# A graph layer on one core: longer lead-in, sets of three groups of two-part rows

## The chip, the cores and the metric

The kernel runs on one core of a Trainium2 chip. A core has TensorE (PE, matrix products; its weight loads are shown apart as PEld), VectorE (DVE), ScalarE (ACT), GpSimd (POOL), SyncE (SP, which here only issues transfers) and 16 DMA engines that move data between the chip's memory and the core's SBUF. Each engine has one queue of instructions and works through it in order; engines wait for one another by semaphores. Sums of matrix products land in PSUM.

The metric is the device time of one execution, in microseconds, as the median of several runs. Before the change it is 2603.83 us (three runs: 2600.77, 2603.83 and 2609.32).

## The reference

One layer of a graph network: 12500 nodes with 256 features, 200000 edges sorted by their target `dst`. All data is float32.

```python
h = relu(layernorm(x))                          # 12500 x 256, over the features
agg = segment_sum(h[src], dst, num_segments=N)  # one sum for each node
z = (1.0 + eps_gin) * h + agg
t = z @ W1 + b1                                 # 256 -> 512
t = relu(batchnorm(t, g1, bt1))                 # over all nodes
y = t @ W2 + b2                                 # 512 -> 256
out = x + relu(batchnorm(y + h, g2, bt2))       # over all nodes
```

The sources `src` are random, so `h[src]` is a gather of 200000 rows of 1 KB. The batch norms need statistics over all nodes, so all of `t` has to be there before the second layer starts.

## The kernel before

**Sizes.** 128 edges make a tile (1563 tiles, the last of 64 edges), 12 tiles (`GT`, L18) make a group (131 groups). Nodes come in 25 chunks of 512. Since `dst` is sorted and the edges are many, the 1536 edges of a group point at some 96 neighbouring nodes (`STEP`, L71), nearly at a place that can be told in advance; `MARGIN` (L19) is the leeway.

**Index part (L134 to L221).** `dst` and `src` are loaded as blocks of 128 x 128 edges, 13 blocks beside each other (L144, L152), all on SP's queue, and cast by DVE (L161). TensorE transposes them (L166) and DVE copies them out (L168), so that each tile's edges lie down a column of `dstT` and `srcT`. L176 to L185 work out, for each group, its first node and each edge's distance to it. Then the kernel checks that all distances are from 0 to 127 and all leeways fit: three passes of DVE per item (L194 clips, L197 compares, L200 counts). The count becomes a flag that is read into a register; 0 leads into `fast()`, 1 into `general()`, which does not run with these inputs.

**Gather and sum (in `fast()`).** `gather(i)` (L378) issues 12 indirect DMAs on POOL's queue (L383), each fetching 128 rows by 128 indices into a buffer `gt`; there are `AHEAD` + 1 = 5 such buffers (L301). `sums(i)` (L404) builds on DVE twelve 128 x 128 matrices `oh`, with a one where an edge points at a node (L408), and TensorE adds up the rows with them: 12 products 128 x 128 by 128 x 256 into one PSUM tile `ps` (L418). That is the sum for 128 neighbouring nodes, which start at the group's first node. `join(i)` (L423) has ACT copy it to SBUF (`zs`, L425) and DVE build a placing matrix `at` (L427); `put(i)` (L432) has TensorE transpose and shift the sum to its place with two products (L437); `add(i)` (L442) has DVE add that to the columns of `z` (L450). A chunk of `z` begins as the columns of `h`, loaded from `h_cols` (SP, L396) and scaled by 1 + eps on ACT (L397). When a chunk is complete, `first_layer(c)` (L453) multiplies it by W1 in four slices of 512 nodes (L459), takes batch statistics on DVE (L463), copies on ACT (L464) and stores the chunk of `t` by one DMA on ACT's queue (L465).

**Lead-in.** The table of normalized rows, `h_tab`, isn't there at the start. The first `LEAD` = 24 groups therefore gather from `x` itself and are normalized in their buffer after the gather: `settle` (L324) takes the statistics of two tiles at a time on DVE (`bn_stats`, L329), the square root on ACT, and normalizes on ACT tile by tile (L340). Beside this, `h_chunk` (L355) normalizes the rows of a chunk in the same manner, stores them to `h_tab` (ACT's queue), transposes them on TensorE (L366) and stores the columns to `h_cols` (SP). From group 24 on, `gather` reads `h_tab`, whose writes must all have landed.

**Order.** A single loop (L472 to L494) goes over the groups: up to two chunks of `h` as they come due, the gather of group i + 4, copy and placing of group i - 1, sums of group i, addition of group i - 1, first layers that are due. The tile scheduler may reorder within what data and buffers allow; each engine then has a fixed queue.

**Second phase (L513 to L558).** Batch norm of `t`, the second layer (L527) from `t_tab`, its statistics, batch norm and output. It starts when the last group is done.

Of the kernel before, what the change touches and what calls it, by code (L numbers as in the profile page):

```python
# [7 lines left out]
F32 = mybir.dt.float32  # L8
I32 = mybir.dt.int32
AF = mybir.ActivationFunctionType  # L10
OP = mybir.AluOpType
# [7 lines left out]
MARGIN = 76  # L19
AHEAD = 4  # L20
LEAD = 24
# [9 lines left out]
def kernel(  # L31
# [41 lines left out]
    NBLK = -(-max(NTILE, NG * GT) // P)  # L73

# [59 lines left out]
    whole_blocks = full_tiles // P  # L134
    rest = NTILE - whole_blocks * P
    with ExitStack() as es:
        raw = es.enter_context(tc.tile_pool(name="raw", bufs=1))
        ps_t = es.enter_context(tc.tile_pool(name="ps_t", bufs=2, space=PSUM))
        ps_v = es.enter_context(tc.tile_pool(name="ps_v", bufs=2, space=PSUM))
        for name, arr in (("d", dst), ("s", src)):  # L140
            ti = raw.tile([P, NBLK, P], I32, name="rawi_" + name)
            tf = raw.tile([P, NBLK, P], F32, name="rawf_" + name)
            if whole_blocks:
                nc.sync.dma_start(  # L144
                    ti[:, :whole_blocks, :],
                    arr[: whole_blocks * P * P].rearrange("(b p e) -> p b e", p=P, e=P),
                )
            if rest:
                nc.gpsimd.memset(ti[:, whole_blocks, :], 0)
                whole = full_tiles - whole_blocks * P  # L150
                if whole:
                    nc.sync.dma_start(  # L152
                        ti[:whole, whole_blocks, :],
                        arr[whole_blocks * P * P : full_tiles * P].rearrange("(p e) -> p e", e=P),
                    )
                if left:
                    nc.sync.dma_start(
                        ti[whole : whole + 1, whole_blocks, :left],
                        arr[full_tiles * P :].rearrange("(o e) -> o e", o=1),
                    )  # L160
            nc.vector.tensor_copy(tf, ti)  # L161
            for b0 in range(0, NBLK, 4):
                m = min(4, NBLK - b0)
                pt = ps_t.tile([P, 4, P], F32, name="pt")
                for b in range(m):
                    nc.tensor.transpose(pt[:, b, :], tf[:, b0 + b, :], ident)  # L166
                to = dstT if name == "d" else srcT
                nc.vector.tensor_copy(  # L168
                    to[:, b0 * P : (b0 + m) * P], pt[:, :m, :].rearrange("p b e -> p (b e)")
                )  # L170
# [15 lines left out]
        held = raw.tile([P, NG * GT], F32, name="held")  # L186
        odd = raw.tile([P, NG * GT], F32, name="odd")
        cnt = raw.tile([P, 3], F32, name="cnt")
        nc.vector.memset(cnt, 0.0)
        parts = [(rel, 0, P, full_tiles, P), (shift, 0, P, NG, 2 * MARGIN + 1)]  # L190
        if left:
            parts.append((rel, full_tiles, left, 1, P))
        for k, (v, t0, rows, n, end) in enumerate(parts):
            nc.vector.tensor_scalar(  # L194
                held[:rows, :n], v[:rows, t0 : t0 + n], 0.0, float(end - 1), op0=OP.max, op1=OP.min
            )
            nc.vector.tensor_tensor(  # L197
                odd[:rows, :n], held[:rows, :n], v[:rows, t0 : t0 + n], op=OP.not_equal
            )
            nc.vector.reduce_sum(cnt[:rows, k : k + 1], odd[:rows, :n], axis=mybir.AxisListType.X)  # L200
        pc = ps_v.tile([P, 3], F32, name="pc")
        nc.tensor.matmul(pc[:1, :], lhsT=ones, rhs=cnt, start=True, stop=True)
        both = raw.tile([1, 3], F32, name="both")
# [61 lines left out]
    def fast():  # L265
# [24 lines left out]
        with ExitStack() as fs:  # L290
# [7 lines left out]

            with ExitStack() as es:
# [46 lines left out]
                def x_chunk(g):  # L346
# [4 lines left out]
                    if n < CH:  # L351
                        nc.vector.memset(xts[g], 0.0)
# [458 lines left out]
```

## Time and profile before

| | |
|---|---|
| median of three runs | 2603.83 us |
| profiled execution, its own time | 2627.44 us |
| its span | 2625.6 us |
| first gather (of `x`) starts | 32.4 us |
| first gather of `h_tab` starts | 504.8 us |
| last gather ends | 2327.6 us |
| busy: PE / PEld / DVE / ACT / POOL | 1404.3 / 1001.2 / 716.2 / 460.3 / 1484.3 us |
| gathers of `x`: 288 | 273.8 us busy, mean 951 ns |
| gathers of `h_tab`: 1275 | 1208.9 us busy, mean 948 ns |

The profile is of one execution. Its own time, 2627.44 us, is longer than the median of the runs, so a sum of its rows is to be set against 2627, not against 2604. Busy time counts an engine's work without its waits. A gather that POOL issues counts only for the time that POOL prepares it; the transfer runs on the DMA engines. Lines are given as L383 and so on; a releaser is what ended the idle time before an instruction, and "remote" there means that the profile found nobody that did.

A view that cuts the 2625.6 us into 40 slices shows how the work is spread: the lead-in is the first seven to eight slices, then POOL is evenly busy to slice 35, and the second phase takes the rest.

```profile
POOL 4654656666666666666666666566666666630000
...
DMA  5444665433333333333333333333333333328728
```

### The profile page before, as it was taken

Reading aid. Unit: us, or ns where it says so; the run is one execution under the profiler, and the core shown is the slowest. Engines: PE = TensorE matmul, PEld = TensorE weight load, DVE = VectorE, ACT = ScalarE, POOL = GpSimd, SP = SyncE. Lnnn points to the kernel's source line nnn. Section 1 sums busy time; section 2 is a strip of 40 time slices with the busy share of each in tenths; the row PEclk is TensorE's granted clock in tenths of the full one; section 3 lists DMA queues with packets and bytes.
Section 4 is the critical chain, followed back from the end, with each engine's and each line's share of the span. In section 5 each row is a group of like instructions: output and inputs, shape, how many; then the busy total and the mean of one; then the engine's idle time right before and its main releaser. Section 6 shows DMA issues by size and latency. Waiting matters only on the chain.

```text
span 2625.6 us, 14777 instructions
## 1 busy us (share of the span) xinstructions
PE 1404.3 (53%) x4873; PEld 1001.2 (38%) x4873; DVE 716.2 (27%) x1060; ACT 460.3 (18%) x871; POOL 1484.3 (57%) x1575
## 2 busy tenths in 40 slices
PE   1234566645455455445545545544555553578995
PEld 1223344434434334343333424433334442453444
DVE  5234555412212112122111212211121211133444
ACT  1335465510000000000000000000000000013434
POOL 4654656666666666666666666566666666630000
PEclk6666777777777777677777767777777776788996
DMA  5444665433333333333333333333333333328728
GB/s 163 158 152 136 206 199 185 139 114 92 116 119 108 100 120 112 92 116 119 113 92 116 112 94 118 105 120 92 119 110 96 116 114 90 108 77 328 273 82 301
DMA packets 150067, 349.41 MB, mean 133 GB/s; under 512 B 28920, under 2 KB 84366, under 8 KB 143838
## 3 DMA queue, kind: packets, MB, share of 16 engines
q0 software_dynamic: 75008, 204.90, 26.9%
q1 hardware_dynamic: 44182, 91.21, 10.0%
q10 hardware_dynamic: 30792, 52.26, 5.3%
q8 instruction: 41, 0.67, 0.1%
q14 instruction: 44, 0.36, 0.0%
HBM read 284.26 MB, written 64.00 MB: 133 GB/s over the span
## 4 chain that ended last, share of the span: by engine, by line
another core or an unknown queue 50%; PE 25%; issue 10%; ACT 6%; DVE 5%; DMA 3%; POOL 1%; ACTq 0%; SPq 0%; DVEq 0%; POOLq 0%
PE ps L418 9%; PE py L527 6%; PE pz L437 4%; PE ph L459 4%; ACT gt L340 3%; DVE st L463 1%; DMA out_dram<-ot 1%; ACT zs L425 1%; POOL gt L383 1%; ACT ht L340 1%; DVE oh L408 1%; PE po L551 1%; ACT zc L397 1%; DMA zc<-h_cols 1%
## 5 line engine op out<-in xcount | busy, mean ns | idle before, releaser
L383 POOL DMA_INDIRECT gt<-h_tab,srcT x1275 | 1208.9, 948 | 616.4 <-issue 373.8
L418 PE MATMUL ps<-gt,oh 128*128 128x256 f32 x3126 | 767.2, 406 | 88.8 <-ACT gt L340 70.8
L418 PEld LDWEIGHTS ps<-gt,oh 128*128 128x128 f32 x3126 | 648.3, 208 | 206.9 <-ACT gt L340 74.3
L437 PE MATMUL pz<-at,zs 128*128 128x280 f32 x524 | 210.8, 538 | 789.1 <-ACT zs L425 672.0
L408 DVE TENSOR_TENSOR oh<-col,dstT 128x1536 f32<-128x1536 f32 x131 | 229.1, 1749 | 1192.6 <-remote 942.9
L437 PEld LDWEIGHTS pz<-at,zs 128*128 128x128 f32 x524 | 121.6, 248 | 850.2 <-ACT zs L425 693.3
L383 POOL DMA_INDIRECT gt<-in_x_dram,srcT x288 | 273.8, 951 | 196.5 <-ACT zs L425 109.3
L425 ACT COPY zs<-ps 128x256 f32<-128x256 f32 x131 | 48.8, 372 | 1614.0 <-remote 1261.3
L459 PE MATMUL ph<-zc,w1s 128*128 128x512 f32 (+1 forms) x400 | 210.3, 677 | 206.2 <-ACT ts L464 138.2
L459 PEld LDWEIGHTS ph<-zc,w1s 128*128 128x128 f32 x400 | 84.9, 220 | 311.6 <-issue 154.9
L450 DVE TENSOR_TENSOR zc<-pz,zc 128x560 f32<-128x560 f32 (+9 forms) x203 | 100.9, 527 | 315.8 <-remote 189.8
L527 PE MATMUL py<-tT,w2s 128*128 128x512 f32 (+1 forms) x400 | 170.9, 591 | 11.7 <-ACT tT L520 11.7
L340 ACT ACTIVATE gt<-gt,nbg,rsg 128x256 f32<-128x256 f32 x288 | 149.5, 590 | 4.2 <-DVE nbg L338 1.9
L527 PEld LDWEIGHTS py<-tT,w2s 128*128 128x128 f32 x400 | 76.9, 193 | 105.7 <-issue 87.2
L463 DVE BATCH_NORM_STATS2 st<-ph 128x6 f32<-128x512 f32 (+1 forms) x100 | 67.1, 681 | 153.5 <-PE ph L459 60.1
L329 DVE BATCH_NORM_STATS2 stg<-gt 128x6 f32<-128x512 f32 x144 | 91.5, 689 | 34.7 <-DMA gt<-in_x_dram,srcT 22.6
L464 ACT COPY ts<-ph 128x512 f32<-128x512 f32 (+1 forms) x100 | 57.4, 575 | 194.9 <-DVE st L463 150.6
L520 ACT ACTIVATE tT<-ti,of,sc 128x512 f32<-128x512 f32 (+1 forms) x100 | 72.1, 791 | 100.8 <-issue 86.7
L366 PE MATMUL pc<-ident,ht 128*128 128x128 f32 x196 | 38.2, 327 | 66.1 <-issue 27.9
L427 DVE TENSOR_SCALAR at<-col,shift 128x280 f32<-128x280 f32 x131 | 65.5, 500 | 0.3 <-PE pz L437 0.3
L531 DVE TENSOR_TENSOR yT<-py,yT 128x512 f32<-128x512 f32 (+1 forms) x50 | 33.9, 678 | 110.2 <-PE py L527 110.2
L366 PEld LDWEIGHTS pc<-ident,ht 128*128 128x128 f32 x196 | 27.7, 168 | 84.9 <-issue 33.8
(74 smaller groups left out, 393.8 us busy)
## 6 DMA issues: line engine op xcount, KB each, us to landing
t_tab<-ts ACTq DMA_DIRECT2D x24, 1024.0 KB
ti<-t_tab SPq DMA_DIRECT2D x24, 1024.0 KB
gt<-h_tab,srcT POOLq DMA_INDIRECT x1275
xt<-in_x_dram SPq DMA_DIRECT2D x24, 512.0 KB
h_tab<-ht ACTq DMA_DIRECT2D x24, 512.0 KB
h_cols<-hc SPq DMA_DIRECT2D x24, 512.0 KB
zc<-h_cols SPq DMA_DIRECT2D x24, 512.0 KB
yT<-h_cols SPq DMA_DIRECT2D x24, 512.0 KB
```

Source lines behind the costliest of these rows:

```text
L329: nc.vector.bn_stats(st[:, c : c + 2, :].rearrange("p c s -> p (c s)"), v[:, c : c + 2, :].rearrange("p c d -> p d c"),)
L340: nc.scalar.activation(to[:, c, :], v[:, c, :], AF.Relu, bias=nb[:, c : c + 1], scale=rs[:, c : c + 1])
L383: nc.gpsimd.indirect_dma_start(out=ga[:rows, t - t0, :], out_offset=None, in_=x if i < LEAD else h_tab, in_offset=bass.IndirectOffsetOnAxi ...
L408: nc.vector.tensor_tensor(oh[:, :n, :], col[:, :P].unsqueeze(1).to_broadcast([P, n, P]), dstT[:, t0 : t0 + n].unsqueeze(2).to_broadcast([P ...
L418: nc.tensor.matmul(ps, lhsT=oh[:rows, j, :], rhs=ga[:rows, j, :], start=(j == 0), stop=(j == n - 1))
L425: nc.scalar.copy(zs, summed.pop(i))
L437: nc.tensor.matmul(pz[:, d, :WIDE], lhsT=zs[:, d * P : (d + 1) * P], rhs=at, start=True, stop=True)
L450: nc.vector.tensor_add(side, pz[:, :, a - lo : b - lo], side)
L459: nc.tensor.matmul(ph[:, :n], lhsT=w1s[:, d, f * P : (f + 1) * P], rhs=zc[c][:, d, :n], start=(d == 0), stop=(d == DC - 1),)
L463: nc.vector.bn_stats(st1[:, f, c, :], ph[:, :n])
L520: nc.scalar.activation(tT[:, f, :n], ti[:, f, :n], AF.Relu, bias=of1[:, f : f + 1], scale=sc1[:, f : f + 1],)
L527: nc.tensor.matmul(py[:, :n], lhsT=w2s[:, f, d * P : (d + 1) * P], rhs=tT[:, f, :n], start=(f == 0), stop=(f == HC - 1),)
```

## The change

1. **Index part.** A partition now holds 13 x 128 = 1664 edges in a row (`PART`) instead of 13 pieces of 128. `dst` is loaded on SP's queue and cast and copied by DVE; `src` is loaded on ACT's queue and cast and copied by ACT. The check takes, in place of three DVE passes, one ACT pass that sums what lies below zero and one DVE maximum.
2. **Two-part rows.** A new table `h_two` (12500 x 512) takes the place of `h_tab` in `fast()`. Each normalized row is stored as `hi`, its value rounded to float32r, and `lo`, the rest (`ht` - `hi`, also float32r). Main groups gather 2 KB rows of it. Their sums run in float32r over 512 columns, one half for `hi` and one for `lo`; `hold` then adds the two (ACT copies `lo`, DVE adds `hi`). The lead-in's groups sum in float32 over 256 columns as before.
3. **Lead-in of 29 groups** (`LEAD`), in an order written out by hand: per group i, the gather of group i + 4, the addition of group i - 4, copy of the sum of i - 2, the one-hots of i + 1, one chunk of `h`, normalizing of gathered group i + 1, sums of i, transposes of chunk i - 1, placing of i - 2, and one slice of the first layer. The first two main groups are gathered in iterations 26 and 27; the lead-in's buffers then give way to those of the main part.
4. **Sets of three** (`SET`) in the main part, also in a fixed order (`manual_schedule`). A set's three sums lie in three parts of one PSUM tile (`pss`), its one-hots in three parts of `ohs`. Per set: for each of the three groups before, copy and add of the halves; then placing and addition one after the other, with the new set's one-hots and up to three slices of the first layer among them; then the three placing matrices; then the three sums, each followed by the gather five groups ahead (`LOTS` = 5 buffers).
5. **Smaller parts.** `MARGIN` 64 instead of 76 (placing matrices of 256 columns instead of 280); two PSUM tiles for placing instead of one; the first layer's slices are copied into three small tiles and stored one by one (100 DMAs instead of 25); loads of `z`'s columns and their scaling are placed by hand.

The diff, cut to its core:

```diff
-MARGIN = 76
+MARGIN = 64
 AHEAD = 4
-LEAD = 24
+SET = 3
+LEAD = 29
...
+        PART = NBLK * P
+        for name, arr, eng in (("d", dst, nc.sync), ("s", src, nc.scalar)):
...
+                eng.dma_start(ti[:safe, :], arr[: safe * PART].rearrange("(p e) -> p e", e=PART))
...
+                if name == "d":
+                    nc.vector.tensor_copy(columns[:, b0 : b0 + m, :], pt[:, :m, :PU])
+                else:
+                    nc.scalar.copy(columns[:, b0 : b0 + m, :], pt[:, :m, :PU])
...
+            nc.scalar.activation(
+                below[:rows, :n], v[:rows, t0 : t0 + n], AF.Relu, bias=zero[:rows], scale=-1.0,
+                accum_out=cnt[:rows, 2 * k : 2 * k + 1],
+            )
+            nc.vector.reduce_max(top[:rows, k : k + 1], v[:rows, t0 : t0 + n], axis=mybir.AxisListType.X)
...
-                held[:rows, :n], v[:rows, t0 : t0 + n], 0.0, float(end - 1), op0=OP.max, op1=OP.min
...
-                odd[:rows, :n], held[:rows, :n], v[:rows, t0 : t0 + n], op=OP.not_equal
...
-            nc.vector.reduce_sum(cnt[:rows, k : k + 1], odd[:rows, :n], axis=mybir.AxisListType.X)
...
+            h_two = dram.tile([N, 2 * D], F32, name="h_two")
...
-                gat = es.enter_context(tc.tile_pool(name="gat", bufs=AHEAD + 1))
...
+                es.enter_context(tc.manual_schedule())
+                LOTS = 5
...
+                ohs = own.tile([P, SET, GT, P], F32R, name="ohs")
+                pss = psp.tile([P, SET, 2 * D], F32, name="pss")
...
+                    hl = lnp.tile([P, R, 2, D], F32R, name="hl")
+                    hi, lo = hl[:, :n, 0, :], hl[:, :n, 1, :]
+                    nc.scalar.copy(hi, ht[:, :n, :])
+                    nc.vector.tensor_tensor(lo, ht[:, :n, :], hi.bitcast(F32), op=OP.subtract)
+                    carry(
+                        nc.scalar, hl.rearrange("p c s d -> p c (s d)").bitcast(F32), h_two, g, store=True,
+                    )
...
-                            out=ga[:rows, t - t0, :], out_offset=None, in_=x if i < LEAD else h_tab,
+                            out=ga[:rows, t - t0, :], out_offset=None, in_=x if i < LEAD else h_two,
...
+                def bank(i):
+                    return pss[:, i % SET, :D] if i < LEAD else pss[:, i % SET, :]
...
+                def hold(i):
+                    zss[i] = sel.tile([P, D], F32, name="zs", bufs=SET)
+                    if i < LEAD:
+                        nc.scalar.copy(zss[i], bank(i))
+                    else:
+                        nc.scalar.copy(zss[i], bank(i)[:, D:])
+                        nc.vector.tensor_add(zss[i], bank(i)[:, :D], zss[i])
...
+                for i0 in range(LEAD, NG + SET, SET):
+                    here = list(range(i0, min(i0 + SET, NG)))
+                    ripe()
+                    some = pick(SET if here else len(done["slices"]))
+                    for i in before:
+                        hold(i)
+                    scale()
+                    ahead = here[i0 == LEAD :]
+                    for k, i in enumerate(before):
+                        put(i)
+                        add(i)
...
+                        if k:
+                            for j in ahead[:1]:
+                                edges(j)
+                            ahead = ahead[1:]
+                            for c, f in some[:1]:
+                                slice_of(c, f)
+                                take(c, f)
+                            some = some[1:]
...
+                    for i in here:
+                        spots(i)
+                    for i in here:
+                        sums(i)
+                        gather(i + LOTS)
+                    if here:
+                        ready(here[-1])
+                    before = here
```

## The prediction

> **What bounds the kernel now.** I read first the page's chain that ended last and its costliest groups, then the span cut into stretches, then the waits inside the long middle stretch, then its timeline.
>
> ```profile
> another core or an unknown queue 50%; PE 25%; issue 10%; ACT 6%; DVE 5%; DMA 3%; POOL 1%; ACTq 0%; SPq 0%; DVEq 0%; POOLq 0%
> ...
> L383 POOL DMA_INDIRECT gt<-h_tab,srcT x1275 | 1208.9, 948 | 616.4 <-issue 373.8
> L418 PE MATMUL ps<-gt,oh 128*128 128x256 f32 x3126 | 767.2, 406 | 88.8 <-ACT gt L340 70.8
> ```
>
> Half of the chain has no named releaser: this kernel is bound by hand-ons that the profile can't place, not by an engine that is full. The stretches:
>
> ```profile
> 32.00:505.00 473.00, 226.22 (x803) 164.32 (x804) 210.53 (x392) 218.53 (x463) 273.97 (x289) 0.69 0.55 176
> 505.00:2328.00 1823.00, 922.82 (x3298) 690.51 (x3298) 372.33 (x473) 125.46 (x242) 1208.69 (x1275) 0.74 0.36 108
> 2328.00:2625.00 297.00, 248.04 (x743) 140.53 (x742) 117.51 (x166) 114.00 (x165) 0.00 (x0) 0.90 0.62 222
> ```
>
> Columns: stretch, length, busy PE, PEld, DVE, ACT, POOL, granted TensorE clock, DMA share, GB/s. Lead-in 473 us (24 groups), middle 1823 us (107 groups, 17.0 us each), second layer and output 297 us. Which engine sets the 17.0 us? The waits from 700 to 2200 us (engine and line, releaser, total, times, longest):
>
> ```profile
> ACT zs L425 <- remote: 981.2, 51, 30.6
> ...
> POOL gt L383 <- issue: 305.5, 1001, 0.6
> POOL gt L383 <- remote: 181.4, 43, 6.4
> ```
>
> Behind each gather POOL spends 0.30 us more (305.5/1001), so a gather takes 0.949 + 0.305 = 1.254 us and a group of 12 takes **15.04 us**. The other 2 us are stalls of 4.2 us (181.4/43), one for each pair of groups: POOL waits for a buffer. The timeline shows why:
>
> ```profile
> 1246.54 7.08 PEld L418 LDWEIGHTS ps<-gt,oh 128*128 128x128 f32 x24
> 1247.00 7.02 PE L418 MATMUL ps<-gt,oh 128*128 128x256 f32 x24
> ...
> 1264.89 0.81 DVE L450 TENSOR_TENSOR zc<-pz,zc 128x344 f32<-128x344 f32 x2 [18.58 <-remote]
> ...
> 1273.40 1.76 DVE L408 TENSOR_TENSOR oh<-col,dstT 128x1536 f32<-128x1536 f32 x1 [7.29 <-remote]
> 1273.45 0.37 ACT L425 COPY zs<-ps 128x256 f32<-128x256 f32 x1 [28.53 <-remote]
> 1273.63 0.95 POOL L383 DMA_INDIRECT gt<-h_tab,srcT  x1 [6.28 <-remote]
> ```
>
> TensorE's 24 records (a group's last 20, the next one's first 4) end at 1254.0. The copy of that sum, the next one-hots and the gather that reuses the buffer need only these matmuls, and all three start at 1273.4, 19 us later. So while gathers run, what TensorE has done is often seen up to some 20 us late; the trace doesn't say by what. Behind the last gather (2327.6) it stops: sums are copied at 2332.2, 2338.3, 2344.5 and 2350.6, 6.1 us a group. The middle is thus POOL's 15.04 us plus the stalls that late hand-ons make. POOL's floor for all 1563 gathers is 1960 us; first to last they take 2295 us, so 335 us are stalls: 112 in the lead-in (473 - 24 x 15.04), 223 in the middle.
>
> **The change part by part**
>
> *Index part.* L194, L197 and L200 (0.97 + 1.79 + 1.78 us) become one ACT pass beside one DVE reduction of 1.8 us, and src's DMAs leave SP's queue for ACT's. The first gather stands at 32.4 us; I put it at 27, which saves 5 (ends 2 and 10).
>
> *Lead-in, 29 groups instead of 24.* A group now takes 472.4/24 = 19.7 us. Added per chunk: the ACT copy that makes hi (1.15 us, as L397 for 1024 elements) and the DVE subtraction that makes lo (1.2 us, as L557), with the stores twice as wide. Both lie on the round trip between DVE statistics and ACT normalizing, so up to +2.4 us a group. Taken away: copy and placing of a sum come two groups later in the engines' queues, and addition four, so POOL's 99.3 us of waits for the copy at L425 (150 to 500 us) can shrink. The slices of the first layer go one to a group, inside the same idle time. I set loss against gain: 19.7 us (ends 15.04, POOL's floor, and 22.1). The 30th group's gathers stand in iteration 26, behind all row stores, and the pools that give way must be done. They start at 27 + 25 (first group gathered and normalized) + 26 x 19.7 = **564 us**. Now they start near 590, so little is won here.
>
> *Gathers of 102 groups from two-part rows.* There are as many gathers, each of 128 rows, with 2 KB a row instead of 1. The trace has no such gather. The nearest row is the last tile: 64 rows, half the bytes, 0.901 us.
>
> ```profile
> L383 POOL DMA_INDIRECT gt<-h_tab,srcT x1275: 901/949/963, 504.8 to 2326.6; - x183
> ```
>
> Halving rows and bytes saves 0.048 us; if bytes alone carry it, doubling them costs 0.096 us, x 1215 = 117 us. The other end is nothing: as many rows are looked up, and more bytes give no gain. I take a quarter, **30 us**[...].
> Will the DMA engines keep up? 262 KB in 1.254 us are 209 GB/s, beside some 16 of other traffic; slices of this profile reach 328. Here a rule of the Trainium skill speaks against the change: DMA: Bandwidth & Descriptors, Anatomy of one DMA, gives a POOL-issued DMA about 2.0 us plus bytes/436 GB/s, so 2.6 us for 262 KB. Paid one after the other this makes 1215 x 2.6 = 3160 us, 1636 over what I sum. But the same rule gives today's gather 2.3 us, and the trace issues one every 1.254 us a thousand times: the fixed part overlaps, only the 0.6 us of bytes counts. I follow the row.
>
> *Sums in float32r.* A float32 matmul is two records (1563 make 3126). Twelve single ones over 512 columns take 12 x 0.216 to 0.427 = 2.6 to 5.1 us a group, if one goes at the pace of today's records (7.02 us for 24: 0.427 at half clock, 0.216 at full). If float32r runs as float32 does, it is 24 records of 512 columns, 10.4 to 20.5 us. I take the first; POOL's 45.1 us for a set hides it. A second rule speaks against it: TensorE: Matmul & The Clock Gate, HAM oscillation, says that idle stretches over some 3.4 us put TensorE back to half clock, and the change leaves it idle longer. The granted clock is 0.74 in the middle already. Wholly at half clock a set costs 15.4 (sums) + 5.1 (placing) + 10.2 (slices) = 31 us, at full 15.5; both lie under 45.1, so neither alters the sum.
>
> *Sets of three, in a fixed order.* Now each group's placing stands in TensorE's queue inside the next group's sums, so every late hand-on holds back a buffer. Afterwards three sums run, then three placings. A set's ring has two hand-ons in series: sums to copy, and first placing to addition, which frees the buffer for the third placing and lets the one-hots follow; work beside them is some 14 us. Five buffers leave POOL 60 us before it needs the first back. At today's mean lateness (981.2 us over 88 groups: 11 us) the ring takes 2 x 11 + 14 = 36 us, under 45.1; at the worst, 2 x 20.2 + 14 = 54. I allow **30 us** of stalls in all (ends 0 and, one stall of 4.3 in each of 34 sets, 146). The margin of 64, the added DVE addition (102 x 0.4 us) and 75 more stores on ACT's queue (0.33 us each) lie on engines busy 20% and 7% of the middle: nothing. Were this cover gone, the ring would lengthen by 1 to 3 us a set, still under 45.1.
>
> *Tail.* From the last gather's end to the end of the span 298 us; kept.
>
> **Sum:** 564 + 1215 x 1.254 (1523) + 30 + 30 + 298 = 2445 us of span, 2447 with the 1.8 us around it, against the profiled execution's 2627.4: **-180 us**. The median of the runs is 2603.8; 180 off it gives 2424.
>
> **Rivals**
> 1. *Main case:* POOL bounds the middle, with few stalls. 2424 us, own range 2330 to 2500. Chance 0.68.
> 2. *Late hand-ons hold the sets (other side).* Place: from a set's last sum to the next set's one-hots. Price: two hand-ons of 20.2 us make 54.4 us a set, 34 x 9.3 = 316 instead of 30 us, 2710. It decides from 5.3 us more a set (180/34). For it: 20 us waits recur. Against it: POOL's stalls end them, and five buffers reach over them. One 4.3 us stall a set gives 2540 (0.07); the full price, or enough of it, 0.08.
> 3. *The wide gather is dearer.* By the linear end 2511 (0.08). Above 0.17 us each (210 us, with the 30 already in) it is slower; the 64-row gather speaks against that (0.05).
> 4. *float32r at float32's pace.* TensorE then needs 31 + 15 = 46 us a set at full clock, and with the ring's waits some 52: 2424 + 34 x 6 = 2630 (0.04).
>
> Within 0.3% is about what a measurement of this kernel can't tell from no change. Faster 0.80, same 0.03, slower 0.17. Range 2330 to 2600: it leaves out half of the lead-in's gain below, and rivals 2 to 4 at full price above.
>
> **What would show it.** Right: gathers of h_two at 0.95 to 1.0 us, POOL stalls in the middle under 100 us, the 30th group starting at 540 to 590, the middle near 15.3 us a group. Wrong: gathers over 1.1 us, POOL waiting some 4 us in every set or more, sums over 6 us a group, or a lead-in beyond 620 us.

## The result, and the profile after

The changed kernel takes 2639.53 us in the median of four runs (2628.70 to 2660.69), the kernel before 2606.57 us (2600.77 to 2618.10). The ratio is **1.0141**, with a 95% interval of 1.0091 to 1.0191: slower by 1.4%, a small loss, where 180 us less were forecast.

The profiled execution of the changed kernel took 2628.70 us, with a span of 2626.8 us. Its stretches, cut at the first main gather and at the end of the last one (columns as in the prediction: stretch, length, busy PE, PEld, DVE, ACT, POOL, granted TensorE clock, DMA share, GB/s):

```profile
26.00:570.00 544.00, 270.83 (x962) 204.42 (x963) 272.33 (x465) 284.68 (x566) 340.03 (x348) 0.76 0.59 189
570.00:2338.00 1768.00, 641.28 (x1976) 431.24 (x1975) 377.77 (x545) 116.43 (x227) 1148.42 (x1215) 0.67 0.66 197
2338.00:2626.00 288.00, 241.52 (x692) 131.64 (x690) 121.81 (x173) 115.54 (x167) 0.06 (x1) 0.90 0.65 233
```

Set beside the sum that was forecast:

| term | forecast, us | measured, us |
|---|---|---|
| start of the first main gather | 564 | 570.1 |
| 1215 main gathers at POOL's own pace | 1523 | 1519 (0.945 + 0.305 us each) |
| wide rows | +30 | 0 |
| stalls in the middle | +30 | **249** (1768 - 1519) |
| behind the last gather | 298 | 289 |
| span | 2445 | 2627 |

The miss is 182 us, and one row, the stalls, is 219 us over its forecast. The costliest groups of the page show that the gathers themselves became no dearer (a mean of 945 ns, against 948 before) and that the sums became cheap:

```profile
L430 POOL DMA_INDIRECT gt<-h_two,srcT x1215 | 1148.5, 945 | 655.5 <-issue 369.0
...
L475 PE MATMUL pss<-gt,ohs 128*128 128x512 f32 x1215 | 348.2, 445 | 136.9 <-issue 98.7
```

What POOL waited for in the middle (POOL's waits from 570 to 2338 us; releaser, total, times, longest) is again its buffers, which the sums set free. The first line is mainly the 0.305 us behind each gather:

```profile
POOL gt L430 <- issue: 369.0, 1147, 18.7
POOL gt L430 <- remote: 131.8, 25, 7.4
POOL gt L430 <- PE pss L475: 110.1, 14, 18.5
```

And the timeline shows that the hand-on from TensorE comes later than it ever did before:

```profile
1216.90 4.25 PE L475 MATMUL pss<-gt,ohs 128*128 128x512 f32 x12 [1.85 <-issue]
...
1261.66 0.94 POOL L430 DMA_INDIRECT gt<-h_two,srcT  x1 [4.33 <-remote]
1281.77 0.37 ACT L484 COPY zs<-pss 128x256 f32<-128x256 f32 x1 [71.67 <-remote]
1282.01 0.94 POOL L430 DMA_INDIRECT gt<-h_two,srcT  x1 [5.65 <-remote]
```

The set's third sum ends at 1221.15. The copy that needs nothing else starts at 1281.77, 60.6 us later. Two stalls of POOL, of 4.33 and 5.65 us, end together with hand-ons: the first lets POOL's own buffer through, the second the copy. Over the 34 sets, the first copy starts up to 62 us after the last sum; before the change the longest lateness in the middle was 22.8 us. That was no fixed bound: stalls of POOL came more often then (54 over 1 us in the middle, 39 after), and hand-ons come through with a stall.

Side by side, the two profiles have the same span for opposite reasons: the first main gather stands 65 us later (570.1 against 504.8, with five groups more in the lead-in), the middle is 55 us shorter (1768 against 1823, with 60 gathers less), and the tail 9 us. Per main gather the middle takes 1823/1275 = 1.430 us before and 1768/1215 = 1.455 us after. The profile of before is of an execution 21 us above its median, that after of one 11 us below, so the 33 us between the medians can't be divided among the stretches.

### The profile page after: what moved, and what is told of

The parts are those of the page before. It is cut to its first block, busy times and chain, and to the rows that moved or that the text cites. A ratio compares the mean times of both kernels' runs of the same rounds, so it can differ in the third digit from the quotient of the medians.

```text
span 2626.8 us, 12696 instructions
## 1 busy us (share of the span) xinstructions
PE 1160.7 (44%) x3658; PEld 773.1 (29%) x3658; DVE 783.2 (30%) x1210; ACT 525.2 (20%) x975; POOL 1491.6 (57%) x1576
## 4 chain that ended last, share of the span: by engine, by line
another core or an unknown queue 32%; issue 22%; PE 20%; DVE 9%; ACT 6%; POOL 6%; DMA 4%; ACTq 0%; DVEq 0%; POOLq 0%
PE py L693 6%; PE pss L475 6%; POOL gt L430 4%; PE ph L514 4%; ACT gx L369 3%; DVE stg L358 3%; PE pz L496 3%; POOL gx L430 2%; DVE ohs L457 2%; DMA gx<-in_x_dram,srcT 2%; DMA out_dram<-ot 1%; DVE zc L507 1%; ACT ht L369 1%; DVE st L525 1%
## 5 line engine op out<-in xcount | busy, mean ns | idle before, releaser
L430 POOL DMA_INDIRECT gt<-h_two,srcT x1215 | 1148.5, 945 | 655.5 <-issue 369.0
L496 PE MATMUL pz<-at,zs 128*128 128x256 f32 x524 | 171.6, 473 | 863.6 <-DVE zs L485 490.2
L430 POOL DMA_INDIRECT gx<-in_x_dram,srcT x348 | 340.0, 977 | 168.2 <-issue 114.8
L475 PE MATMUL pss<-gt,ohs 128*128 128x512 f32 x1215 | 348.2, 445 | 136.9 <-issue 98.7
L475 PE MATMUL pss<-gx,ohs 128*128 128x256 f32 x696 | 216.9, 485 | 282.1 <-ACT zs L482 164.7
L475 PEld LDWEIGHTS pss<-gt,ohs 128*128 128x128 f32 x1215 | 255.3, 213 | 225.2 <-issue 151.0
L475 PEld LDWEIGHTS pss<-gx,ohs 128*128 128x128 f32 x696 | 172.0, 252 | 336.7 <-ACT zs L482 180.9
L457 DVE TENSOR_TENSOR ohs<-col,dstT 128x1536 fp32r<-128x1536 f32 x131 | 226.5, 1736 | 0.0
L369 ACT ACTIVATE gx<-gx,nbg,rsg 128x256 f32<-128x256 f32 x348 | 174.1, 587 | 14.5 <-DVE nbg L367 9.5
L358 DVE BATCH_NORM_STATS2 stg<-gx 128x6 f32<-128x512 f32 x174 | 107.7, 685 | 11.3 <-DMA gx<-in_x_dram,srcT 11.3
```

Of the source, the lines that this page charges most:

```text
L358: nc.vector.bn_stats(st[:, c : c + 2, :].rearrange("p c s -> p (c s)"), v[:, c : c + 2, :].rearrange("p c d -> p d c"),)
L369: nc.scalar.activation(to[:, c, :], v[:, c, :], AF.Relu, bias=nb[:, c : c + 1], scale=rs[:, c : c + 1])
L430: nc.gpsimd.indirect_dma_start(out=ga[:rows, t - t0, :], out_offset=None, in_=x if i < LEAD else h_two, in_offset=bass.IndirectOffsetOnAxi ...
L457: nc.vector.tensor_tensor(ohs[:, i % SET, :n, :], col[:, :P].unsqueeze(1).to_broadcast([P, n, P]), dstT[:, t0 : t0 + n].unsqueeze(2).to_br ...
L475: nc.tensor.matmul(bank(i), lhsT=oh[:rows, j, :], rhs=ga[:rows, j, :], start=(j == 0), stop=(j == n - 1))
L496: nc.tensor.matmul(pz[:, d, :], lhsT=zs[:, d * P : (d + 1) * P], rhs=at, start=True, stop=True)
```

## The experiments

All of them were held against these theories:

- **A**: while POOL gathers, each hand-on from TensorE is late by itself; a pause of POOL lets it through.
- **B**: the 2 KB rows load the DMA engines and hold things up.
- **C**: TensorE's last update stays behind until TensorE goes on with other work.
- **D**: five buffers are too few, whatever the hand-ons do.
- **E**: the number of hand-ons counts, at a fixed rate.
- **F**: what gathers lead to is worked off at a rate of its own, one in some 1.42 us; POOL issues one in 1.25 us, and TensorE is held up by the surplus. **G**: the same, by the number of gathers and not by their rows.
- **H**: the stalls come from TensorE's own amount of work.

Each experiment is one execution with a profile. Four executions of the changed kernel differ by up to 1.2%, so smaller differences in time say little; the middles of its two profiles agree within 3 us. "Middle" is from the start of the first main gather to the end of the last, and "stalls" is what it takes above POOL's own pace. The kernel before, run beside them on the same chip, took 2594.8 us (first four runs), 2602.8 (next four), 2613.6 (next three), 2266.5 (next four) and 2592.6 us (last three).

### Width of the rows, a pause, no gathers, a busy TensorE

**half_rows.** Main gathers of 1 KB: the low parts of the rows are left out.

```diff
-            h_two = dram.tile([N, 2 * D], F32, name="h_two")
+            h_two = dram.tile([N, D], F32, name="h_two")
...
-                    carry(
-                        nc.scalar, hl.rearrange("p c s d -> p c (s d)").bitcast(F32), h_two, g, store=True,
-                    )
+                    carry(nc.scalar, hl[:, :, 0, :].bitcast(F32), h_two, g, store=True)
...
-                        gathered[i] = pools[k >= 2].tile([P, GT, 2 * D], F32R, name=f"gt{k >= 2:d}")
+                        gathered[i] = pools[k >= 2].tile([P, GT, D], F32R, name=f"gt{k >= 2:d}")
...
-                        nc.scalar.copy(zss[i], bank(i)[:, D:])
-                        nc.vector.tensor_add(zss[i], bank(i)[:, :D], zss[i])
+                    nc.scalar.copy(zss[i], bank(i))
```

> Main groups gather only the hi half: 1 KB rows, sums over 256 columns, one ACT copy; lo is left out of the sums. Theory A (what TensorE finishes is seen late as long as POOL issues gathers back to back, whatever their width; only a stall of POOL lets it through): POOL's stalls in the middle stay near the 248 us of the changed kernel, 2600 to 2640 us, and copies of sums still come tens of us after the last sum. Theory B (the 2 KB rows load the DMA engines and hold things up): stalls fall under 80 us, 2400 to 2460 us.

Measured: 2603.2 us. The middle takes 1765 us, 243 of them above POOL's own pace, and copies still come up to 63 us after the last sum. That is theory A's number; theory B falls. The width may cost something elsewhere: the first main gather stands at 548.9 us, some 20 us earlier than with the wide stores (570.1, and 574.1 in after_again). But the bfloat16 kernels below, whose rows are as narrow, start it at 555 to 587 us, so this isn't shown.

**pool_pause.** POOL does something else for a while behind each set's gathers.

```diff
                     for i in here:
                         sums(i)
                         gather(i + LOTS)
+                    if here:
+                        for _ in range(12):
+                            nc.gpsimd.memset(pad, 0.0)
```

> POOL fills a scratch tile 12 times (about 6 us) behind the gathers of each set of three, 34 sets, 204 us of added POOL work. Theory A, if only gathers do harm: what TensorE did comes through during each pause, POOL's waits for buffers in the middle fall from 248 to under 60 us, 2560 to 2620 us. Theory A, if any work of POOL does it: waits stay, 2780 to 2830 us. Theory B (width of the rows) says nothing of the pause: waits shrink only by what overlaps, 2700 to 2830 us.

Measured: 2629.1 us, neither of the two times for theory A. The pauses of 7.1 us take the place of the waits one for one: POOL's waits for buffers fall to one of 8.5 us, besides one of 18.8 us at the start, and the middle still takes 1764 us. The work that POOL does in a pause counts as rest from gathering. The time, however, is as if the sum of pauses were fixed.

**sp_loads.** The same bytes by SP's queue.

```diff
+                        if i >= LEAD:
+                            r0 = t * 61 % (N - P)
+                            nc.sync.dma_start(ga[:rows, t - t0, :], h_two[r0 : r0 + rows, :])
+                            continue
                         nc.gpsimd.indirect_dma_start(
```

> The main groups are loaded as 128 consecutive rows of the two-part table by SP's queue, one DMA a tile of the same 262 KB, in place of POOL's gathers; which rows are summed is thus not the reference's. Theory A: without POOL's gathers the copy of a set's sums follows its last sum within 3 us throughout, however full the DMA engines are. Theory B: with the same bytes in flight, copies still come more than 10 us after the last sum.

Measured: 2004.4 us. In the waits from 700 to 1700 us the copy of the sums (L488 there) has a named releaser, the sums, and no "remote" at all:

```profile
ACT zs L488 <- PE pss L479: 192.9, 28, 9.2
```

Every copy starts as the set's last product ends. The DMA engines moved 260 GB/s in the mean here, against 198 with gathers. So it isn't full DMA engines that hold TensorE up. The loads differ from the gathers in two things, though, the queue and the rows, which are consecutive and not scattered; the run doesn't tell which of the two counts.

**busy_pe.** TensorE goes on behind the third sum.

```diff
+                        for _ in range(24):
+                            nc.tensor.matmul(
+                                idle, lhsT=w1s[:, 0, :P], rhs=w1s[:, 0, :D], start=True, stop=True
+                            )
                         ready(here[-1])
```

> Behind a set's third sum TensorE makes 24 more products into an unused part of PSUM (48 records of 256 columns, 10 to 20 us), so that it doesn't fall idle with the last sum. Theory C (TensorE's last update stays behind until TensorE goes on): the copy of the sums starts while these products run, within 5 us of the last sum, and POOL's stalls in the middle fall under 100 us, 2440 to 2530 us. Theory A: copies still wait for a stall of POOL, tens of us after the last sum, stalls 220 to 350 us, 2600 to 2730 us.

Measured: 2906.1 us, slower than any theory had it. The copies come at once now, in all sets but one near the start; POOL stalls some 15 us in every set, as the ring has become longer. But the next hand-on is late: the first placing ends at 1229.6 us, TensorE works on until 1234.3, and the addition starts at 1263.9, behind a stall of POOL. So theory C falls.

### Order, buffers, spacing, depth

**early_onehots.** The one-hots ahead of the additions in DVE's queue.

```diff
-                    ahead = here[i0 == LEAD :]
+                    for j in here[i0 == LEAD :]:
+                        edges(j)
...
-                            for j in ahead[:1]:
-                                edges(j)
-                            ahead = ahead[1:]
```

> In the changed kernel, DVE builds the next set's one-hots right behind the copies of the sums, ahead of the additions, which wait for TensorE's placing. Theory A (late hand-ons from TensorE while POOL gathers): the next sums no longer queue behind a second late hand-on on DVE's queue, stalls of POOL in the middle fall from 260 to 120 to 200 us, 2500 to 2570 us. Theory D (five buffers are too few whatever the hand-ons do): 2620 to 2650 us.

Measured: 2627.2 us; 231 us of stalls are left. That misses A's number and meets D's, which the next run tests.

**before_8_buffers.** The kernel before with eight buffers, and main gathers seven groups ahead.

```diff
+MAINAHEAD = 7
...
-                gat = es.enter_context(tc.tile_pool(name="gat", bufs=AHEAD + 1))
+                gat = es.enter_context(tc.tile_pool(name="gat", bufs=2 * AHEAD))
```

> The kernel before, with eight gather buffers in place of five and main gathers seven groups ahead. Theory A: a late hand-on lasts until POOL stalls, so more buffers only put the same stalls off; 2570 to 2610 us, stalls of POOL in the middle still 180 to 240 us. Theory D: POOL runs through the late hand-ons, stalls under 80 us, 2430 to 2480 us.

Measured: 2660.5 us, middle 1815 us, 221 of stalls. Theory D falls for the kernel before. (The 58 us above the kernel before are not in the middle, which took 1823 us in the profile of before.)

**spaced_gathers.** A small fill behind each main gather.

```diff
+                        if i >= LEAD:
+                            nc.gpsimd.memset(pad[:, :P], 0.0)
```

> Changed kernel with a small fill by POOL (128 elements, some 0.2 us) behind each of the 1215 main gathers; POOL's floor grows by 240 to 600 us. If it is the rate of gathers that holds TensorE's hand-ons back: copies follow the last sum within 3 us, no stall over 1 us is left but for a few, total 2627 - 250 + the added fill. If only a pause of several us frees them: late copies of tens of us and stalls stay, total 2627 + most of the fill.

Measured: **2570.2 us**, less than any run of either kernel where TensorE is held up: POOL was given 1215 instructions more and the end came sooner. A gather and its fill take 1.34 us in the median, so POOL's own pace is 105 us slower, and the stalls over 1 us fall from 261 us to 107. Copies are still late by up to 48 us. A middle of 1721.5 us, 1.417 us a gather.

**bf16_deep.** Rows as two bfloat16 parts, ten buffers, a ring of four groups.

```diff
-SET = 3
+SET = 2
+SLOTS = 4
...
-                LOTS = 5
+                LOTS = 10
...
-                pss = psp.tile([P, SET, 2 * D], F32, name="pss")
+                pss = psp.tile([P, SLOTS, D], F32, name="pss")
```

> Rows as two bfloat16 parts in 1 KB (hi and lo, added into the same 256 columns), ten gather buffers, sums and one-hots in a ring of four groups, and a main loop in which no engine waits for a product of TensorE made less than one set of two groups (30 us) before. Theory A, if a hand-on is late by some 10 to 30 us on its own: stalls under 60 us, 2400 to 2460 us. Theory A, if TensorE's updates get through at a fixed rate of one in some 10 us while POOL gathers: 2.8 updates a group don't fit in 15 us, stalls stay near 2 us a group, 2580 to 2640 us. Theory D: 2400 to 2460 us.

Measured: 2644.3 us, stalls of 211 us, 1.424 us a gather. That looked like theory E. The run was no fair test of A, though: all slots of the ring lay in one tile, and the copies waited for the newest sum in it.

### The number of hand-ons

**more_updates.** Two more hand-ons a set.

```diff
+                        spare = [ps_h.tile([P, CH], F32, name="ph") for _ in range(2)]
+                        for k in range(2):
+                            nc.tensor.matmul(
+                                spare[k][:, :2], lhsT=w1s[:, 0, :P], rhs=w1s[:, 0, :2], start=True, stop=True
+                            )
+                        for k in range(2):
+                            nc.scalar.copy(more[:, 2 * k : 2 * k + 2], spare[k][:, :2])
                     for i in before:
                         hold(i)
```

> Changed kernel, plus two tiny products a set behind the third sum, each of two columns, each copied by ACT ahead of the copies of the sums; so TensorE hands on 11 times a set instead of 9. Theory E (while POOL gathers, TensorE's updates get through at a limited rate, some 5.8 us each over the whole run: 52.4 us for 9 a set, 34.4 for 5.5 or 6 before and in the deep kernel): +11.6 us a set, 33 sets, 2627 + 380 = about 3000 us. Theory A (a hand-on is late by itself, and the number doesn't matter): the two ride with the last sum's hand-on, at most 1 us a set, 2620 to 2680 us.

Measured: 2627.1 us. Theory E asked for 380 us more, and falls; A's number is met.

**deep_6_updates** (four hand-ons a set, as its expectation says, not six) and **deep_2_updates**: the deep kernel with a tile for each set, and the latter with shared tiles inside a set. The first pair of lines is against bf16_deep, the rest is deep_2_updates against deep_6_updates.

```diff
-                pss = psp.tile([P, SLOTS, D], F32, name="pss")
+                pss += [psm.tile([P, 2, D], F32, name=f"pss{k}") for k in range(2)]
...
-                        gathered[i] = ga = pools[k].tile([P, GT, 2 * D], BF16, name=f"gt{k:d}", bufs=(6 if k else 4))
+                            lots[0] = pools[k].tile([P, SET, GT, 2 * D], BF16, name=f"gt{k:d}")
+                        gathered[i] = ga = lots[0][:, (i - LEAD) % SET]
```

> The deep bfloat16 kernel with each set's sums, placings, slices and one-hots in tiles of their own, so that copies really wait only for the set before (in bf16_deep they waited for the newest sum in the shared tile); TensorE hands on 4 times in a set of two groups, gathers wait group by group. Theory A (late by 10 to 60 us each): covered by the ring of two sets where the lateness is under 30 us; 2430 to 2560 us. Theory E: 4 x 5.8 = 23 us for a set of 30, no stalls, 2420 to 2470 us.

> The same, but both groups of a set gathered into one tile, both placings and both slices in one tile each, so that a set hands on 2 to 3 times instead of 4. Theory E: 2.5 x 5.8 = 15 us for a set of 30, no stalls beyond those of the start, 2410 to 2450 us. Theory A: as deep_6_updates or later by up to 15 us a set, since buffers come free set by set: 2430 to 2600 us.

Measured: 2604.2 and 2634.6 us; stalls of 204 and 222 us; 1.418 and 1.433 us a gather. With ten buffers and a ring that can wait for tens of us, the stalls stay, so theory D falls for the changed kernel too, and A's picture of single late messages doesn't hold either. The timeline of deep_6_updates shows why. TensorE's rows (start, length, what, idle before):

```profile
1415.80 4.86 PE L487 MATMUL pss<-gt,ohs 128*128 128x256 bf16 x43
1421.40 0.27 PE L487 MATMUL pss<-gt,ohs 128*128 128x256 bf16 x1 [0.74 <-issue]
...
1441.70 0.37 PE L487 MATMUL pss<-gt,ohs 128*128 128x256 bf16 x1 [1.73 <-issue]
1444.50 0.37 PE L487 MATMUL pss<-gt,ohs 128*128 128x256 bf16 x1 [2.43 <-issue]
1447.30 0.37 PE L487 MATMUL pss<-gt,ohs 128*128 128x256 bf16 x1 [2.43 <-issue]
...
1459.90 3.36 PE L487 MATMUL pss<-gt,ohs 128*128 128x256 bf16 x15 [0.33 <-issue]
```

POOL had stalled until 1409.35 us. For some 11 us TensorE runs through 43 products in 4.9 us. Then, with gathers still coming every 1.25 us, the same kind of product starts only every 2.1 to 2.8 us, in steps of some 0.70 us. It isn't waiting for rows: by the DMA packets of this trace, the last packet of a gather comes at most 4.2 us after POOL is done with it (700 to 2200 us; 4.8 us in the profile after), and POOL is several groups ahead. POOL's next stall begins at 1454.0; at 1459.9 TensorE is fast again. The windows on TensorE say the same (stretch, length, busy PE, granted clock, DMA share, GB/s). The granted clock of 0.50 isn't the reason: at half clock products start 0.427 us apart instead of 0.227 in the profile after, and here they are some twenty times slower:

```profile
1410.00:1420.00 10.00, 10.00 (x56) 0.90 0.58 184
1430.00:1454.00 24.00, 4.36 (x11) 0.50 0.36 107
```

So it is not the message alone that is late: **TensorE itself is held up** while gathers come too closely.

### Rate, rows or TensorE's work

**rows_64, one_product, spaced_more and before_spaced** ran on the chip where the kernel before takes 2266.5 us.

```diff
-                        rows = left if t == full_tiles else P
+                        rows = left if t == full_tiles else P if i < LEAD else P // 2
```

> Changed kernel, main gathers and their sums with 64 rows instead of 128: as many gathers, half the rows; the other half of the edges is left out. Theory F (what a gather leads to takes some 1.42 us by the number of its rows, while POOL issues one every 1.25 us; TensorE is held up while that is worked off): 64 rows stay far below that, no late copies, POOL runs at 0.90 + 0.30 us, stalls under 60 us, middle about 1490 us, total 2350 to 2390 us. Theory G (the number of gathers matters, not their rows): 2560 to 2630 us, stalls near 250 us.

```diff
+                    n = n if i < LEAD else 1
                     for j in range(n):
```

> Changed kernel, all gathers kept, but only the first of a group's twelve products is made, the other eleven tiles don't enter the sums. Theory H (the stalls come from TensorE's own work, which gets done only in the short times around POOL's stalls): two thirds of TensorE's work in the middle are gone, stalls fall under 120 us, 2450 to 2500 us. Theories F and G: stalls stay above 180 us, 2560 to 2640 us.

```diff
+                        if i >= LEAD:
+                            nc.gpsimd.memset(pad[:, : 2 * P], 0.0)
```

> As spaced_gathers, with the fill of 256 elements: a gather every 1.45 us or more. Theories F and G: above 1.42 us nothing piles up any more; copies follow the last sum within 3 us, almost no stall over 1 us but those that a fill waits for DVE, and the middle takes 1740 to 1820 us, total 2580 to 2670 us. Theory H: late copies and some stalls stay.

> The kernel before with the fill of 128 elements behind each main gather. Theories F and G: the hand-ons come sooner as in spaced_gathers, where stalls of 261 us became 107; floor +105 us, stalls 223 to about 90 us: 2560 to 2600 us. Theory H: the same stalls beside a higher floor, 2650 to 2720 us.

Measured: 2228.8, 2284.1, 2518.4 and 2616.0 us. On this chip nothing is held up in any of them, not even with a gather every 1.25 us: in one_product POOL waits for its buffers not once from 484 to 2002 us, apart from the 9.2 us of the start,

```profile
POOL gt L430 <- issue: 356.9, 1172, 0.3
POOL gt L430 <- DMA gt<-h_two,srcT: 11.6, 38, 0.3
POOL gt L430 <- PE ph L405: 9.2, 1, 9.2
```

and the middle takes 1518.0 us, POOL's own pace to the microsecond. The lead-in's gathers, too, end at 476 us instead of 534. The four runs therefore tell no theory from another, and rows_64 leaves open whether rows or gathers count. In before_spaced the scheduler moreover put the fills together in 22 pauses of 7.5 us instead of one behind each gather, so it isn't what it was to be; it is 350 us slower than the kernel before there, of which these pauses make 165, and the rest stays unexplained.

**after_again, one_product_2 and spaced_more_2** met a chip on which TensorE is held up (kernel before 2592.6 us).

> The changed kernel once more, beside the kernel before on the same chip. If TensorE is held up there (before at 2595 to 2615 us): 2620 to 2660 us, late copies of tens of us. If it isn't (before near 2266 us): no stall of POOL over 1 us in the middle, first main gather at 484 us, middle 1518 us, end 285 us behind it, 2280 to 2295 us, so about 1% slower than before there too, and 140 us or so below the 2424 of the prediction.

> Changed kernel, one product of twelve in each main group, all gathers kept (eleven tiles don't enter the sums). Where TensorE is held up, theory H (TensorE gets its work done only around POOL's stalls, so less work needs fewer stalls): stalls of POOL in the middle under 120 us, 2450 to 2500 us. Theory F (gathers are worked off at one in some 1.42 us whatever TensorE does): stalls above 180 us, 2560 to 2640 us. Where it isn't held up: 2284 us as in one_product.

> Changed kernel with the fill of 256 elements behind each main gather, at least 1.45 us from one gather to the next. Where TensorE is held up, theory F: above 1.42 us nothing piles up, copies within 3 us, hardly a stall, middle 1740 to 1820 us, 2580 to 2670 us. Theory H: late copies and stalls stay above 60 us. Where it isn't held up: 2518 us as in spaced_more.

Measured: after_again 2643.4 us (middle 1770.6), which repeats the first profile. one_product_2 2584.1 us: with a twelfth of the sums' products the middle still takes 1712.6 us, 191 above POOL's own pace; after_again has 247 above it. Theory H falls as the main cause; F's numbers are met. TensorE's work may account for up to 56 us. spaced_more_2 2624.1 us: here the gathers come every 1.448 us, and from 700 to 2200 us the waits of POOL and of the copies are

```profile
ACT zs L487 <- PE pss L478: 1010.3, 24, 46.2
...
POOL gt L431 <- issue: 172.3, 1036, 0.9
```

No "remote" is left: in no set does the first copy start more than 0.04 us after the last sum, and POOL doesn't stall. The same kernel without the fill, on the same chip, has 259 us of stalls over 1 us.

All runs on chips that hold TensorE up, middle per main gather in us:

| kernel | POOL's own pace | measured |
|---|---|---|
| before; before_8_buffers | 1.25 | 1.430; 1.424 |
| after; after_again | 1.25 | 1.455; 1.457 |
| half_rows, pool_pause, more_updates, early_onehots | 1.25 | 1.453, 1.452, 1.445, 1.440 |
| bf16_deep, deep_6_updates, deep_2_updates | 1.25 | 1.424, 1.418, 1.433 |
| one_product_2 | 1.25 | 1.410 |
| spaced_gathers | 1.34 | 1.417 |
| spaced_more_2 | 1.45 | 1.448 |

Only busy_pe, whose own ring is longer, lies outside (1.665). Whatever the row width, the order, the buffers or TensorE's work: no middle is shorter than 1.41 us a gather. That is the rate of theories F and G. What serves it, and why one chip doesn't show it, these runs don't tell; the rows themselves land in time.

One rival stands untested: the recording of the profile itself. For each gather the trace has 16 packets of 4 bytes, and on the chip without hold-up there is a record of a semaphore's update for each such packet (one_product, 700 to 1900 us: 16547 packets, 16545 records). On the others most of these records are missing while gathers run at full pace:

| run, 700 to 1900 us | packets of 4 bytes | records of updates by DMA |
|---|---|---|
| before | 13822 | 3126 |
| after | 14372 | 2617 |
| one_product_2 | 14855 | 1755 |
| spaced_more_2 (1.45 us a gather) | 14302 | 10431 |
| sp_loads (no gathers) | 19865 | 19875 |

Behind the last gather they are complete in before and after. So the recording falls behind where TensorE is held up, and in part in spaced_more_2, where it isn't. Whether it causes this, or suffers from the same thing, no run tells, as every execution here was recorded; nor is it shown that TensorE is held up without a profile. It also means that "remote" in these traces can be a record that is missing. The late starts stand: of the 1215 products of the main sums none is missing.

## Why the prediction was wrong

**Right.** The first gather starts at 26.2 us (27 forecast). The first main gather starts at 570.1 (564 forecast), though the balance of loss and gain that I assumed is not shown to be the reason; in the variants on the chip without the hold-up it stands at 484. The wide gather costs nothing (30 allowed, ends 0 and 117). The Trainium skill's DMA: Bandwidth & Descriptors, Anatomy of one DMA, whose 2.0 us plus bytes would have made 3160 us if taken one after another, was rightly set aside for the row: gathers still started every 1.25 us. Float32r products start 0.227 us apart at full clock and 0.427 at half (1209 to 1221 us), 2.7 to 5.1 us a group (2.6 to 5.1 forecast), so rival 4 didn't come. TensorE's clock in the middle fell from 0.74 to 0.67, the way that the rule on idle stretches pointed (0.50 from 1225 to 1260 us, with TensorE idle); busy 641 of 1768 us, TensorE had room for it, as the cover said. The tail is 289 us (298).

**Wrong: "Sets of three, in a fixed order", the allowance of 30 us of stalls.** It measured 249 us. The step took the hand-ons for messages that are late by 11 us in the mean and 20.2 at worst, put two of them into a ring of 36 to 54 us and set this against 45.1 us of gathering and 60 us of buffers. The 11 us are ACT's wait at L425, which begins before the sum is done; from the end of a sum to its copy it is 8.2 us in the mean of the middle's 107 groups. The 20.2 us were no worst case: 22.8 occurred before, and with stalls further apart the lateness became 62. The step before it had the same flaw: "The middle is thus POOL's 15.04 us plus the stalls that late hand-ons make" reads the stalls as the effect of one order of work, to be had back by another. The experiments put a rate in its place: 17.0 us a group is 12 gathers at 1.42 us. Sets of three, ten buffers, fewer hand-ons and a twelfth of the products all end near there. Rival 2 had the right place and its deciding point was passed (6.4 us more a set than summed, (249 - 30)/34, against 5.3), but it was given 0.15 in all, since I held that POOL's stalls end the lateness and five buffers reach over it. Stalls and pauses do end it, but their sum is what the rate asks for, so another order of work doesn't shorten it. What sets the rate stays open.

The sum with the right term: 570 + 1215 x 1.455 + 289 = 2627. The change moves 60 gathers into the lead-in, which grows by 65 us, and takes 60 x 1.430 = 86 us from the middle; the other 1215 stay at their rate, 0.025 us dearer each (30 us). So this change won nothing where TensorE is held up.

Where it isn't, there was probably nothing to win either. The kernel before takes 2266.5 us there, and that leaves no room for stalls: 32 us to the first gather and 1563 gathers at 1.254 us = 1960, both as in the profile of before, leave 274 us behind them. The changed kernel itself had no run on that chip. Its variant one_product took 2284.1 us; with its first main gather at 484 us, its middle of 1518 and a tail of 285, an estimate for the changed kernel is 2287 us, 0.9% more than before.

The profile of before had a sign of the rate: a stall of POOL is the longer, the more gathers lie between it and the stall before. In the middle the median is 2.26 us after 12 gathers (10 stalls), 4.37 us after 24 (35) and 6.25 us after 36 (8), of which 0.305 us are there behind any gather. The rest is 0.16 to 0.17 us a gather, and 1.25 + 0.17 is 1.42. (In deep_6_updates 27 stalls after 36 gathers have a median of 6.27 us; in the profile after, single stalls don't follow this.) Here is one after 24 gathers and one after 12; the next, after 36, is the 6.28 us at 1273.63 that the prediction shows.

```profile
1205.53 0.95 POOL L383 DMA_INDIRECT gt<-h_tab,srcT  x1 [4.32 <-remote]
...
1222.51 0.95 POOL L383 DMA_INDIRECT gt<-h_tab,srcT  x1 [2.26 <-remote]
```

## What to carry to other kernels

When an engine's stalls recur, set the length of each against the number of its instructions since the last one, and divide the stretch by their number, before explaining the stalls one by one: a constant time per instruction over different orders of work is a rate. Then test it by slowing that engine down a little; where a surplus is what hurts, the slower pace costs nothing (2570.2 us with 1215 fills more, 2602.8 for the kernel before on the same chip; one run of each, so a gain that is not confirmed). A lateness seen in one profile is no upper bound as long as it isn't known what ends it. And where waits have no releaser, count whether the trace holds the records that would name one.

## What the runs showed of the hardware

- While POOL issues indirect gathers of 128 rows every 1.25 us, TensorE is held up on four of five chips in the profiled runs: its hand-ons come up to 62 us late, and products that otherwise start 0.11 us apart start 2.1 to 2.8 us apart. In the stretch shown of deep_6_updates this began some 11 us after the gathers went on. In the stretches shown of before, after and deep_6_updates it ended with a stop of the gathers of 2.3 to 6.3 us. It doesn't appear with gathers every 1.45 us, nor with plain loads by SP's queue at a higher rate of bytes (260 against 198 GB/s). The Trainium skill (Perfetto Trace Analysis, Tensor Engine Instruction) has a product's update follow PSUM's acknowledgement, and says that a product's end in a profile is estimated; so where only ends are seen, the trace can't tell a late product from a late message. The late starts in deep_6_updates are no such estimate.
- It differs between chips, or between the times at which they were met: of the five chips that the experiments met, each in one batch of runs, four held TensorE up and one didn't, and there the kernel before takes 2266.5 us instead of 2592.6 to 2613.6.
- A pause of 12 fills of 0.58 us on POOL took the place of the stalls (a middle of 1764 against 1768 us); 2 KB rows cost POOL no more than 1 KB rows (945 against 948 ns).
- Where TensorE is held up, the trace lacks most records of semaphore updates (2617 for 14372 packets in the profile after, 16545 for 16547 on the chip without hold-up).
